# A state-space convolution block on one core: the first output product ahead of the depthwise products, copies of u on ScalarE, and one in_proj visit a pair

## The chip, the cores and the metric

The kernel runs on one core of a Trainium2 chip. The metric is the device time of one execution in microseconds. The core has five engines that run side by side: TensorE (matrix products into eight PSUM banks), VectorE, ScalarE, GpSimd (called Pool here) and SyncE, which issues the DMAs. In the profile they are PE (and PEld for its weight loads), DVE, ACT, POOL and SP.

## The reference

x has the shape (4, 128, 96, 96). It is normalized in 32 groups of channels. Four sequences are then made of every image (rows forward, rows backward, columns forward, columns backward), each goes through the same block, and the four results are put back in place, joined, mixed by a last matrix and added to x:

```python
t = _grouped1x1(x, in_proj_w, in_proj_b, G)
u, gate = (t[:, :HID], t[:, HID:])
u = jax.nn.silu(u)
u = lax.conv_general_dilated(u, dw_w, ..., feature_group_count=HID)   # 5 taps along the sequence
s = _conv1x1(u, ssm_in_w)
a = DMIN + (DMAX - DMIN) * jax.nn.sigmoid(_conv1x1(u, ssm_delta_w, ssm_delta_b))
bb = jnp.tanh(_conv1x1(u, ssm_b_w, ssm_b_b))
cc = jnp.tanh(_conv1x1(u, ssm_c_w, ssm_c_b))
prefix = jnp.cumsum(jnp.log(a), axis=-1)
hst = jnp.exp(prefix) * jnp.cumsum(bb * s * jnp.exp(-prefix), axis=-1)
u = u + _conv1x1(cc * hst + ssm_d[None, :, None] * s, ssm_out_w)
u = _grouped1x1(u * jax.nn.sigmoid(gate), mix_w, mix_b, G)
return _conv1x1(u, out_proj_w, out_proj_b)
```

HID is 256, MH (the width of the state) 32, and a sequence is 9216 long. `hst` is the recurrence h = a h + bb s.

## The kernel before, in words

**Tiling.** A sequence is cut into steps of 16 lines, and each step into four interleaved planes of 384 elements (`N`). A *unit* is one plane of one step of one direction; a *pair* is the two units of the forward and the backward direction, s = 0 and 1, that are worked on together. There are 8 phases (4 images, columns "V" and rows "H"), 6 steps in each and 4 pairs in a step: 192 pairs, t = 0 to 191, and k = t % 4. In the second half of a phase the two directions meet values that the first half has made, so gates and activations are read back from DRAM there.

**The order is written by hand.** Each engine runs its instructions in the order of the program, and the program emits them pair by pair: `pair(t)` for the first six, `pair_on(t)` for the others, then `tail()`. In pair t the front half works on units 2t and 2t + 1 (taps, depthwise products, projections), and the back half on the pair n = t - 6 (`bi` = 2n), whose recurrence is done by then: its ssm_out products, its gating, and, one pair later still, its output products. Everything of one pair is in this order on TensorE:

1. the depthwise products of the first 128 channels, `conv` (band matrices, tile `band`, line 730), into banks 6 and 7;
2. the first output product, `add_next(w[0])` with `accumulate` (line 938, tile `w_fin`), 16 matmul instructions into bank 4; ScalarE copies it to a tile `ys` (line 946, or 944 where a bias is added), and Pool adds that into the accumulator `acc` (line 963). It belongs to the pair before: its operand is the gated v of that pair;
3. in the pairs with k = 0 and 1 ("doubles") the rest of the depthwise products, `conv_less` (tile `less`), into banks 6 and 7 again. In the pairs with k = 2 and 3 ("singles") an addition of an edge row on VectorE (`add_lone`, line 775) takes their place;
4. the second output product, into bank 5;
5. the gate products of the next pair (`gate`, line 630) or the in_proj products of a later step (`new_front`'s `one`, line 492), into banks 4 to 7, mixed with the four `ssm_out` products (`out_of`, line 650) into banks 0 to 3;
6. the projections `proj` (tile `main`), into banks 4 and 5.

**The copies of u.** `under(bi, s)` (line 662) is a ScalarE copy of the unit's u into the two ssm_out banks (0 and 1 for s = 0, 2 and 3 for s = 1), so that the ssm_out product adds to it. A unit that has had this copy is in `seeded`; for others `gating` has an additional VectorE addition (line 710). `gating` (line 711) multiplies the sum by the gate. Banks 0 and 1 are shared with the sum of the taps (`taps`, line 828 on VectorE; the first tap is a ScalarE instruction, line 826), so the taps of one pair, `under(bi, 0)`, the product and the gating take turns in them.

**The early pairs.** In pairs 1 to 5 u is copied out of PSUM by two VectorE copies (line 1012). The in_proj products of the third step come in whole visits, `whole_front(f)`: four products, two Silu instructions (line 505), one over two banks (line 516) and four DMAs of the staged rows (line 523). Visit 8 is in pair 4, visits 9 and 10 in pair 5, and both visits of pair 5 use the banks 6, 7, 2 and 3.

In a phase's course ScalarE's other steps of a pair are the gate's tanh (lines 666, 672) or the Silu of in_proj, and those of `proj`: lines 865, 868, 874 and 886 (`scale_s`).

Of the kernel before, what the change touches and what calls it, by code (L numbers as in the profile page):

```python
# [56 lines left out]
R = 4  # L57
LN = 16
NS = HH // LN
N = LN * WW // R  # L60
# [9 lines left out]
def conv_preact_kernel(  # L70
# [9 lines left out]
    nc = tc.nc  # L80
# [41 lines left out]
    psum = ps.tile([P, 8, 512], F32, name="psum")  # L122
    SSM, TAPS, PROJ = 0, 0, (4, 5)
    FRONT = (7, 6, 2, 3)

    def bank(i):
        return psum[:, i, :]
# [238 lines left out]
    def less_of(p):  # L366
        return 1 if p < 2 else 0
# [172 lines left out]

    def whole_front(i, banks):
        one = new_front(i, banks)
        for s, j in ((0, 1), (0, 0), (1, 0), (1, 1)):
            one(s, j)
        new_silu(i, banks)
        new_stage(i, banks)
        new_rest(i)
# [94 lines left out]
    def ssm(bi, s):  # L642

        k = bi - NU + 8 + s
        return turning[k % 3] if bi >= NU - 8 else SSM + 2 * s
# [13 lines left out]
    def under(bi, s):  # L659

        seeded.add((bi, s))
        nc.scalar.copy(psum[:, ssm(bi, s) : ssm(bi, s) + 2, :N], us[bi][:, s])  # L662
# [50 lines left out]
    us = {}  # L713
# [7 lines left out]
    def blocks(step):  # L721
        return [sils[step][:, s if fresh(step) else 1 - s, 0] for s in range(2)]

    def conv(i, banks, alone=False):

        step, p = units[i]["step"], units[i]["p"]
        sil, k, b0 = blocks(step), less_of(p), min(banks)
        for s in range(2):
            for g in range(4):
                mm(bank(b0 + s), g, band[:, s, p, g, :], columns(step, sil[s][:, g, :], 1 - k),  # L730
                   True, alone)

    def alone(p):
        return p in (0, R - 1)
# [244 lines left out]
    def piece(t, place):  # L979
        later.pop((t % NP, place), lambda: None)()  # L980

    waiting, held = [], []
# [14 lines left out]
    def pair(t):  # L997
        i = 2 * t
        banks = head_banks(t)
        if t == R:  # L1000
            load_lone(1)
        if t:
            new_u(i)
            taps(i, range(1, K))
            single = alone(units[i]["p"])
            conv(i, banks, single)
            if single:
                add_lone(i, banks)
            else:
                conv_less(i, banks, False)  # L1010
                for s in range(2):
                    nc.vector.tensor_copy(us[i][:, s, 0, :], bank(min(banks) + s)[:, :N])
            first_tap(i + 2)
            spots = FRONT if banks == PROJ else (5, 4, 2, 3)
            if t < R:
                front(t + R, spots)
            for f in {4: (8,), 5: (9, 10)}.get(t, ()):
                whole_front(f, (4, 5, 2, 3) if banks != PROJ else (6, 7, 2, 3))
        recurrence(t)
        stats_chunks(t)  # L1020
        load_chunks(t + 2)
        proj(i, banks)
        n, s = divmod(t, 2)
        if n < 2:
            for j in range(2):
                gate(2 * n, s, j, 2 + j)
            for j in range(2):
                tanh_one(n, tile_of(n), s, j, 2 + j)
            load_gate(2 * n + s + UB)
        if t < 2:  # L1030
            keep_silu(0, t)
        if t > 3:
            nc.sync.dma_start(keep(t - 4), tile_of(t - 4))
        if t > 0:
            s = tbs[i - 2][0:64, :]
            nc.gpsimd.tensor_scalar(s, s, d_sb[0:64, 0:1], None, ALU.mult)

    def pair_on(t):
        i, k, n, end = 2 * t, t % R, t - LAG, NU // 2
        bi, last = 2 * n, t == end - 1  # L1040
        late = n > 1 and (n - 1) % (NP * 2) == 0
# [15 lines left out]
        banks, w = (6, 7), PROJ  # L1057
        adder = (nc.vector, True) if last else ()
# [3 lines left out]
            lone[un["step"]] = lone[un["step"] - 1]  # L1062
        elif k == 0 and un["st"] > NS // 2:
            load_lone(un["step"])
        under(bi, 1)
        if k in (1, 3) or late:
            for b, at in reload:
                nc.sync.dma_start(planes(accf, at), planes(xr[b], at))
# [3 lines left out]
        new_u(i)  # L1072
        taps(i, range(1, K))
        conv(i, banks, single)
        if single:
            add_lone(i, banks)
        recurrence(t)
# [4 lines left out]
        for add in held:  # L1082
            add()
        held.clear()
        def add_next(bk):
            if n:
                add = accumulate(waiting.pop(0), bk, *adder)
                held.append(add) if late or k == R - 1 and not last else add()

        add_next(w[0])  # L1090
        if not single:
            conv_less(i, banks, False)
        under(bi, 0)
        if not single:
            copy_u(i, banks)
        add_next(w[1])
        spots = (6, 7, 4, 5)
        if ahead is not None:
            one = new_front(ahead, spots)
# [13 lines left out]
        out_of(bi, 1, 0)  # L1113
        gate_of(0, 1, 5)
        piece(t, 1)
        for s in range(2):
            gating(bi, s)
            if s == 0 and gated is not None:
                for x, y in ((1, 4), (0, 5)):
                    if gated % NP > 1:  # L1120
                        tanh_one(gated, to, x, 1, y)
                    else:
                        spot = to[:, (1 - x - shift) % 5]
                        tanh_into(gated, spot, 1, bank(y)[:, :N])
                        nc.sync.dma_start(keep(gated)[:, x, 1], spot)
            elif s == 0 and ahead is not None:
                new_silu(ahead, spots)
# [335 lines left out]
```

## Time and profile before

| | |
|---|---|
| median of 3 runs | 1733.81 us (1731.57 to 1736.02) |
| the profiled execution | 1736.02 us, span 1734.3 us |
| granted TensorE clock, mean | 0.998 |
| TensorE busy | 1706.6 us |
| VectorE busy | 1506.4 us |
| ScalarE busy | 1479.8 us |
| Pool busy | 1478.3 us |
| HBM read and written | 197.77 MB and 126.70 MB, 187 GB/s over the span |

The span runs from the first to the last instruction of the program; the run's time has 1.7 us around it. A line of the timeline gives the start, the length, the engine, the source line, the operation, the tiles written and read, and how many instructions were merged; in brackets stands the idle time of the engine ahead of it and what ended it. An instruction's length on TensorE is modelled, and the lengths of neighbours overlap, so the distance from one group's start to the next says how long a group takes. A group line has the count after x, then busy time and mean length in ns, then the idle time ahead. Each fp32 matmul appears as two instructions, so four 32-column products into one bank and their second halves give 8 rows, and an output product 16.

### The profile page before, as it was taken

Reading aid. Unit: us, or ns where it says so; the run is one execution under the profiler, and the core shown is the slowest. Engines: PE = TensorE matmul, PEld = TensorE weight load, DVE = VectorE, ACT = ScalarE, POOL = GpSimd, SP = SyncE. Lnnn points to the kernel's source line nnn. Section 1 sums busy time; section 2 is a strip of 40 time slices with the busy share of each in tenths; the row PEclk is TensorE's granted clock in tenths of the full one; section 3 lists DMA queues with packets and bytes.
Section 4 is the critical chain, followed back from the end, with each engine's and each line's share of the span. In section 5 each row is a group of like instructions: output and inputs, shape, how many; then the busy total and the mean of one; then the engine's idle time right before and its main releaser. Section 6 shows DMA issues by size and latency. Waiting matters only on the chain.

```text
span 1734.3 us, 50199 instructions
## 1 busy us (share of the span) xinstructions
PE 1706.6 (98%) x20410; PEld 703.5 (41%) x20410; DVE 1506.4 (87%) x1508; ACT 1479.8 (85%) x2435; POOL 1478.3 (85%) x1455
## 2 busy tenths in 40 slices
PE   7999999999999999999999999999999999999998
PEld 3343344434443434444444434444344433444333
DVE  6799998888889999888888989988888888888897
ACT  4788888888888888888888888888888888888875
POOL 3589898888889988988888988989888889998887
PEclk9999999999999999999999999999999999999999
DMA  7755885358994788337797488733899538753474
GB/s 241 208 169 163 281 242 146 131 197 261 287 289 152 232 245 246 124 132 251 238 306 232 154 275 239 216 117 126 253 287 288 192 119 275 227 167 116 132 239 169
DMA packets 143140, 362.63 MB, mean 209 GB/s; under 512 B 19264, under 2 KB 85696, under 8 KB 142912
## 3 DMA queue, kind: packets, MB, share of 16 engines
q1 hardware_dynamic: 142768, 359.39, 66.7%
q8 instruction: 162, 2.65, 0.7%
q14 instruction: 66, 0.54, 0.1%
q10 hardware_dynamic: 144, 0.04, 0.0%
HBM read 197.77 MB, written 126.70 MB: 187 GB/s over the span
## 4 chain that ended last, share of the span: by engine, by line
PE 89%; DMA 4%; DVE 3%; ACT 2%; issue 1%; POOL 0%; SPq 0%; ACTq 0%; DVEq 0%; POOLq 0%
PE psum L131 72%; PE psum L650 6%; PE psum L630 5%; PE psum L492 5%; DMA kept<-shared 2%; DVE psum L828 1%; DMA sil<-shared 1%; DMA sil<-sil 1%; DVE t L903 1%; DVE u L711 1%; ACT psum L826 1%; DMA acc<-in_xr 0%; PE psum L1274 0%; ACT psum L662 0%; ACT shared L516 0%
## 5 line engine op out<-in xcount | busy, mean ns | idle before, releaser
L828 DVE SCALAR_TENSOR_TENSOR psum<-sil,small,psum 128x768 f32<-128x768 f32 x576 | 589.2, 1023 | 51.6 <-ACT psum L826 34.0
L131 PE MATMUL psum<-u,w_fin 128*32 128x384 f32 (+1 forms) x6192 | 554.6, 485 | 1.1 <-ACT ys L944 0.5
L131 PE MATMUL psum<-u,main 128*32 128x384 f32 x6144 | 537.1, 490 | 1.2 <-ACT shared L672 0.6
L711 DVE SCALAR_TENSOR_TENSOR u<-gate,psum 128x768 f32<-128x768 f32 x376 | 341.9, 951 | 137.9 <-PE psum L650 65.0
L963 POOL TENSOR_TENSOR acc<-ys,acc 128x384 f32<-128x384 f32 x375 | 441.5, 1199 | 12.5 <-ACT ys L944 1.9
L131 PEld LDWEIGHTS psum<-u,w_fin 128*32 128x32 f32 x6192 | 203.1, 109 | 307.9 <-issue 209.3
L131 PEld LDWEIGHTS psum<-u,main 128*32 128x32 f32 x6144 | 180.2, 110 | 328.7 <-issue 207.3
L662 ACT COPY psum<-u 128x768 f32<-128x768 f32 x384 | 306.2, 798 | 7.1 <-DVE u L711 4.3
L909 POOL TENSOR_TENSOR t<-t,t 64x384 f32<-64x384 f32 (+1 forms) x192 | 261.8, 1364 | 45.6 <-DVE t L903 30.8
L131 PE MATMUL psum<-sil,band 128*32 128x384 f32 x3072 | 288.3, 486 | 4.4 <-ACT shared L516 2.2
L876 POOL TENSOR_SCALAR t<-tm 64x384 f32<-64x384 f32 x191 | 180.8, 947 | 125.3 <-ACT tm L865 113.4
L650 PE MATMUL psum<-t,main 32*128 32x384 f32 x1536 | 272.1, 519 | 3.7 <-ACT psum L662 3.0
L910 POOL TENSOR_TENSOR t<-t,t 64x384 f32<-64x384 f32 (+1 forms) x192 | 237.5, 1237 | 15.1
L877 POOL TENSOR_TENSOR t<-t,tm 64x384 f32<-64x384 f32 x192 | 235.6, 1227 | 15.3
L828 DVE SCALAR_TENSOR_TENSOR u<-sil,small,psum 128x768 f32<-128x768 f32 x192 | 194.9, 1015 | 6.8
L946 ACT COPY ys<-psum 128x384 f32<-128x384 f32 x288 | 138.3, 480 | 56.9 <-PE psum L131 46.9
L826 ACT ACTIVATE psum<-sil,small 128x768 f32<-128x768 f32 x191 | 171.7, 899 | 17.5 <-DVE u L711 13.4
L131 PEld LDWEIGHTS psum<-sil,band 128*32 128x32 f32 x3072 | 106.7, 109 | 153.2 <-issue 71.1
L630 PE MATMUL psum<-x_in,wn 32*128 32x384 f32 x768 | 161.0, 497 | 0.0
L492 PE MATMUL psum<-x_in,wn 32*128 32x385 f32 x704 | 149.4, 504 | 2.2 <-ACT sil L505 2.2
L505 ACT ACTIVATE sil<-psum,bnorm 128x385 f32<-128x385 f32 x176 | 102.4, 583 | 48.7 <-PE psum L492 35.5
L666 ACT ACTIVATE gate<-psum,bnorm 128x384 f32<-128x384 f32 x168 | 97.3, 581 | 43.5 <-PE psum L630 25.3
(112 smaller groups left out, 1692.6 us busy)
## 6 DMA issues: line engine op xcount, KB each, us to landing
gate<-kept SPq DMA_DIRECT2D x106, 768.0 KB, 5.6
kept<-gate SPq DMA_DIRECT2D x82, 768.0 KB, 3.7
sil<-sil SPq DMA_DIRECT2D x32, 770.0 KB, 7.9
sil<-shared SPq DMA_DIRECT2D x240, 96.2 KB, 2.8
x_in<-in_xs SPq DMA_DIRECT2D x194, 96.2 KB, 3.2
out<-acc SPq DMA_DIRECT2D x46, 384.0 KB, 7.7
x_in<-in_xs SPq DMA_DIRECT2D x88, 192.5 KB, 5.4
acc<-in_xr SPq DMA_DIRECT2D x39, 384.0 KB, 6.9
```

Of the source, the lines that this page charges most:

```text
L131: nc.tensor.matmul(o[r, : rhs.shape[-1]], lhsT, rhs, start=start, stop=stop, skip_group_check=True)
L492: nc.tensor.matmul(bank(banks[2 * j + s])[:, : N + 1], stats[units[step * UB]["b"]][0][a, s, :], x_in[s][a, q, :], start=True, stop=True,)
L630: nc.tensor.matmul(bank(to)[:, :N], stats[un["b"]][0][r, s, :], x_in[s][r, q, off : off + N], start=True, stop=True)
L650: nc.tensor.matmul(bank(ssm(bi, s) + j)[:, :N], w_so[r, bass.ts(j, P)], z[r, :], start=(bi, s) not in seeded, stop=True, skip_group_check= ...
L662: nc.scalar.copy(psum[:, ssm(bi, s) : ssm(bi, s) + 2, :N], us[bi][:, s])
L711: nc.vector.scalar_tensor_tensor(v, g, 1.0, pz, ALU.add, ALU.mult)
L826: nc.scalar.activation(part, src, AF.Copy, scale=w_tap[:, 0:1])
L828: nc.vector.scalar_tensor_tensor(us[i][:, :, 1, :] if k == K - 1 else part, src, w_tap[:, k : k + 1], part, ALU.mult, ALU.add,)
L877: nc.gpsimd.tensor_mul(ta[0:64, p, :], tb[0:64, :], tm[0:64, :])
L909: engine.tensor_mul(ta[0:64, p, r], tb[64:P, r], ta[64:P, p, r])
L910: engine.tensor_add(tb[0:64, r], ta[0:64, p, r], tb[0:64, r])
L963: adder.tensor_add(part, y, part)
```

## The change

Five things are changed.

- A whole visit issues its four in_proj products in the order (0,1), (1,1), (0,0), (1,0) of (s, j).
- In pairs 4 and 5 one ScalarE copy over two banks takes u out of PSUM, in place of two VectorE copies; pairs 1 to 3 keep these.
- Pairs 4 and 5 have one visit each (8 and 9). Visit 10 moves to pair 6, the first of `pair_on` (n = 0), behind its depthwise products, with the banks 4, 5, 2 and 3. That pair leaves out `under(bi, 1)`, since banks 2 and 3 are in use, and so has the additional VectorE addition for s = 1.
- From pair 7 to 190 the first output product is issued at the very start of the pair, ahead of `under(bi, 1)` and of the depthwise products, into bank 2. Only its matmuls and its copy to `ys` move; `settle` issues Pool's addition where it was. The last pair keeps the old place and bank 4.
- Ahead of the gating VectorE copies one column of u (128x1) onto itself.

```diff
@@ whole_front
-        for s, j in ((0, 1), (0, 0), (1, 0), (1, 1)):
+        for s, j in ((0, 1), (1, 1), (0, 0), (1, 0)):
             one(s, j)
@@ pair
             else:
                 conv_less(i, banks, False)
-                for s in range(2):
-                    nc.vector.tensor_copy(us[i][:, s, 0, :], bank(min(banks) + s)[:, :N])
+                if t < R:
+                    for s in range(2):
+                        nc.vector.tensor_copy(us[i][:, s, 0, :], bank(min(banks) + s)[:, :N])
+                else:
+                    nc.scalar.copy(us[i][:, :, 0, :], psum[:, min(banks) : min(banks) + 2, :N])
             first_tap(i + 2)
             spots = FRONT if banks == PROJ else (5, 4, 2, 3)
             if t < R:
                 front(t + R, spots)
-            for f in {4: (8,), 5: (9, 10)}.get(t, ()):
-                whole_front(f, (4, 5, 2, 3) if banks != PROJ else (6, 7, 2, 3))
+            if t >= R:
+                whole_front(t + R, (4, 5, 2, 3) if banks != PROJ else (6, 7, 2, 3))
@@ pair_on
-        under(bi, 1)
+        def add_next(bk):
+            return accumulate(waiting.pop(0), bk, *adder) if n else None
+
+        def settle(add):
+            if add:
+                held.append(add) if late or k == R - 1 and not last else add()
+
+        first = None if last else add_next(2)
+        if n:
+            under(bi, 1)
...
         conv(i, banks, single)
+        if not n:
+            whole_front(t + R, (4, 5, 2, 3))
         if single:
             add_lone(i, banks)
...
         held.clear()
-        def add_next(bk):
-            if n:
-                add = accumulate(waiting.pop(0), bk, *adder)
-                held.append(add) if late or k == R - 1 and not last else add()
-
-        add_next(w[0])
+        if last:
+            first = add_next(w[0])
+        settle(first)
         if not single:
             conv_less(i, banks, False)
         under(bi, 0)
         if not single:
             copy_u(i, banks)
-        add_next(w[1])
+        settle(add_next(w[1]))
...
         piece(t, 1)
+        corner = us[bi][:, 0, 0, 0:1]
+        nc.vector.tensor_copy(corner, corner)
         for s in range(2):
             gating(bi, s)
```

## The prediction

> **What bounds the kernel now.** I read the spans and clocks first, then the page and the list of waits, then the timeline of single pairs, because the first views leave little to find.
>
> ```profile
> core 0: 1734.3 us, clock 0.998
> ```
> ```profile
> PE 1706.6 (98%) x20410; PEld 703.5 (41%) x20410; DVE 1506.4 (87%) x1508; ACT 1479.8 (85%) x2435; POOL 1478.3 (85%) x1455
> ...
> PE 89%; DMA 4%; DVE 3%; ACT 2%; issue 1%; POOL 0%; SPq 0%; ACTq 0%; DVEq 0%; POOLq 0%
> ```
> ```profile
> PE psum L131 <- ACT shared L672: 2.6, 4, 1.3
> PE psum L131 <- ACT shared L516: 2.2, 6, 1.0
> ```
>
> TensorE is busy for 98% of the span and carries 89% of the chain that ended last. The waits that the list gives it are few: 2.6 and 2.2 us, at the start of a pair's depthwise products. But a busy TensorE is modelled with overlapping ends, so a short wait between two groups does not show as idle time. It shows in the distance from one group to the next. Here is one pair in full (pair 11, the second of two "single" pairs), from one pair's projections to the next.
>
> ```profile
> 115.78 2.79 PE L131 MATMUL psum<-u,main 128*32 128x384 f32 x32
> ...
> 118.39 1.48 PE L131 MATMUL psum<-sil,band 128*32 128x384 f32 x16
> ...
> 119.68 2.77 PE L131 MATMUL psum<-u,w_fin 128*32 128x384 f32 x32
> ...
> 119.73 0.62 ACT L886 ACTIVATE t<-t,small 64x384 f32<-64x384 f32 x1
> ...
> 120.26 0.79 ACT L662 COPY psum<-u 128x768 f32<-128x768 f32 x1
> ...
> 120.53 1.01 DVE L828 SCALAR_TENSOR_TENSOR u<-sil,small,psum 128x768 f32<-128x768 f32 x1
> ...
> 121.22 0.48 ACT L946 COPY ys<-psum 128x384 f32<-128x384 f32 x1 [0.17 <-PE psum L131]
> ...
> 121.59 0.81 ACT L662 COPY psum<-u 128x768 f32<-128x768 f32 x1
> ...
> 122.37 0.58 PE L630 MATMUL psum<-x_in,wn 32*128 32x384 f32 x1
> ...
> 122.54 0.60 PE L650 MATMUL psum<-t,main 32*128 32x384 f32 x3
> ...
> 123.58 1.82 DVE L711 SCALAR_TENSOR_TENSOR u<-gate,psum 128x768 f32<-128x768 f32 x2 [0.18 <-PE psum L650]
> ...
> 124.04 2.79 PE L131 MATMUL psum<-u,main 128*32 128x384 f32 x32
> ...
> 124.68 0.90 ACT L826 ACTIVATE psum<-sil,small 128x768 f32<-128x768 f32 x1
> ```
> A "double" pair (one with the `less` products), two pairs earlier, for the same place:
> ```profile
> 105.94 0.58 PE L630 MATMUL psum<-x_in,wn 32*128 32x384 f32 x1
> ...
> 105.94 0.60 PE L650 MATMUL psum<-t,main 32*128 32x384 f32 x3
> ...
> 107.52 2.79 PE L131 MATMUL psum<-u,main 128*32 128x384 f32 x32
> ```
>
> In the double pair the gate product (L630) and the three ssm_out products (L650) start together and the projections follow 1.58 us later. In the single pair L650 starts 0.17 us after L630 and the projections follow 1.67 us after. What L650 waits for stands just above: ScalarE's second copy of u into the ssm_out banks (L662, `under(bi, 0)`) ends at 121.59 + 0.81 = 122.40. So a single pair (8.26 us from 115.78 to 124.04) is set by ScalarE, and it is 0.09 us over what TensorE needs. ScalarE in turn loses 0.17 us in that pair, waiting with its copy of the first output product (L946), which stands between the two copies of u. That idle time is what the reordering can remove.
>
> There is a second thread into the same copy. `under(bi, 0)` writes banks 0 and 1, where the taps are summed, so it also waits for VectorE's last tap, which ends at 120.53 + 1.01 = 121.54, 0.05 us before the copy starts. The same two events in pair 10 (the first single pair), and in pair 51, where the output products' copy adds a bias:
>
> ```profile
> 112.19 1.01 DVE L828 SCALAR_TENSOR_TENSOR u<-sil,small,psum 128x768 f32<-128x768 f32 x1
> ...
> 113.33 0.81 ACT L662 COPY psum<-u 128x768 f32<-128x768 f32 x1
> ```
> ```profile
> 471.47 1.01 DVE L828 SCALAR_TENSOR_TENSOR u<-sil,small,psum 128x768 f32<-128x768 f32 x1
> ...
> 472.15 0.59 ACT L944 ACTIVATE ys<-psum,b_fin 128x384 f32<-128x384 f32 x1 [0.17 <-PE psum L131]
> ...
> 472.63 0.81 ACT L662 COPY psum<-u 128x768 f32<-128x768 f32 x1
> ...
> 473.31 0.59 PE L492 MATMUL psum<-x_in,wn 32*128 32x385 f32 x1
> ...
> 473.58 0.60 PE L650 MATMUL psum<-t,main 32*128 32x384 f32 x3
> ```
>
> Tap to copy: 113.33 - 113.20 = 0.13 us, and 472.63 - 472.48 = 0.15 us. With the bias L650 is 0.27 us late, because the copy takes 0.59 instead of 0.48.
>
> **The first output product ahead (pairs 7 to 190; pair 191 keeps the old order).** Sixteen matmuls (about 1.29 us, 118.39 to 119.68) move from behind the depthwise products to ahead of them, from bank 4 to bank 2, and their copy moves ahead of both copies of u. TensorE's work is the same. New waits: the product needs bank 2, which the second gating of the pair before reads until 123.58 + 1.82 = 125.40, while TensorE comes free at 124.04 + 2.61 = 126.65. It doesn't wait; everything of TensorE would queue behind it. The copy to ys needs the product, ready near 118.39 + 1.48 = 119.87, while ScalarE ends L886 only at 120.35: no wait either, and both copies of u stand behind it. The pair's add of the edge row now follows depthwise products that end at 119.68 + 1.48 = 121.16, before the tap at 121.54 lets VectorE go. The Pool adds keep their place, no DMA is moved, and ys has four buffers.
>
> So ScalarE's 0.17 us go and the copy can start earlier, until the tap holds it. How soon after a tap a waiting ScalarE starts is seen in the early rows below: 66.41 + 1.01 = 67.42 to 67.46, that is 0.04. Left to gain are then 0.13 - 0.04 = 0.09 in the first single pair, 0.05 - 0.04 = 0.01 in the second, and TensorE's own pace allows 0.09. Of 88 single pairs (7 to 183), 24 have the bias (two of four in the second half of each H phase, 12 fours). The other 32 fours: 32 x 0.10 = 3.2 us. With the bias I take 0.17 (ScalarE's idle) in the first and 0.15 - 0.04 = 0.11 in the second: 12 x 0.28 = 3.4. Bounds for these two terms: nothing, if another ScalarE step fills the hole; and 88 x 0.09 plus 24 x 0.10 (0.27 against 0.17 of lateness) = 10.3, if the tap moves up too. I take 6.6, what the tap leaves.
>
> **Waits at the start of a pair.** The 4.8 us of the two waits in the list above lie ahead of the depthwise products, because ScalarE still reads banks 6 and 7. The first output product now runs in that time (1.29 us covers all but the longest). But where ScalarE is very late it is late again at the end of the pair, as in the pair with the 1.3 us wait:
>
> ```profile
> 1036.50 0.81 ACT L662 COPY psum<-u 128x768 f32<-128x768 f32 x1
> ...
> 1037.45 0.60 PE L650 MATMUL psum<-t,main 32*128 32x384 f32 x3
> ```
>
> L650 starts 0.14 after the copy ends at 1037.31, so that pair returns only ScalarE's hole, 0.2 us, and so does the one with 1.0. The rest, 2.5 us, I count in full: 2.9 us, between 0.4 and 4.8.
>
> **Pairs 4 to 6.** Here the span has its worst stretch.
>
> ```profile
> 65.11 0.88 PE L131 MATMUL psum<-sil,less 64*32 64x384 f32 x16
> ...
> 66.41 1.01 DVE L828 SCALAR_TENSOR_TENSOR u<-sil,small,psum 128x768 f32<-128x768 f32 x1
> ...
> 67.46 0.91 ACT L826 ACTIVATE psum<-sil,small 128x768 f32<-128x768 f32 x1 [2.43 <-DVE u L828]
> ...
> 69.03 2.92 PE L492 MATMUL psum<-x_in,wn 32*128 32x385 f32 x8 [2.18 <-ACT sil L505]
> ...
> 71.88 4.65 PE L131 MATMUL psum<-u,main 128*32 128x384 f32 x32
> ...
> 72.03 0.58 ACT L505 ACTIVATE sil<-psum,bnorm 128x385 f32<-128x385 f32 x1 [0.74 <-PE psum L492]
> ...
> 72.52 0.90 ACT L516 ACTIVATE shared<-psum,bnorm 128x770 f32<-128x770 f32 x1
> ...
> 80.88 2.79 PE L131 MATMUL psum<-u,main 128*32 128x384 f32 x32
> ```
> ```profile
> 68.90:75.60 6.70, 6.57 (x32) 2.20 (x36) 5.39 (x5) 3.30 (x6) 2.87 (x3) 0.50 0.92 259
> ```
>
> Pair five's second visit of in_proj waits 2.18 us for the first one's banks, the granted clock is then 0.50 for 6.7 us (the eighth column of the stretch), and 32 projections take 4.65 us instead of 2.79. After the change pair five has one visit. ScalarE copies u (0.8) as soon as the `less` products end, near 66.2 with ScalarE's longer queue of pair four (its copy of 0.8 now stands ahead of the first tap; VectorE in return is freed of two copies). So the projections of pair five start near 67.1, not 71.88, and end near 69.8. The depthwise products of pair six follow (1.5), then the moved visit (0.9), near 72.2. Its first two products go to banks 2 and 3, free by then. ScalarE then has two L505 (0.58), one L516 (0.90) and the one copy left of pair six (0.81), about 2.6 us after 72.1: 74.8. L650 follows, and the projections 1.5 us later at 76.4, against 80.88: 4.5 us. The four sil DMAs of the visit are issued in pair six behind pair five's stores of gates; they are first read by pair eight, about 10 us on. The copy that pair six leaves out (ScalarE 0.8) comes back as an add on VectorE between the two gatings, like one L711 of 1.82 / 2 = 0.91. That pushes pair seven's taps past the 0.21 us that VectorE has there, and costs 0.6: net 3.9 us, between 1.2 (no half clock in another run) and 4.5.
>
> The Trainium skill, in "TensorE: Matmul & The Clock Gate" (the practical table at its end), says that the clock stays up unless TensorE idles for about 3 us. By that rule the gap would not have halved the clock; here 2.18 us of idle time stood right before it, so the measurement decides, and the shorter gap left in pair six is a risk, below.
>
> **The corner copy.** One VectorE copy of 128x1 a pair, ahead of the gating, on 186 pairs. The nearest row:
>
> ```profile
> L243 DVE COPY mean<-psum 128x1 f32<-128x1 f32 x3 | 0.5, 152 | 0.0
> ```
>
> VectorE idles 0.18 us just there (the row of 123.58), waiting for L650, and the corner waits only for the copy of u that ended at 122.40. So I take nothing. Below nothing it can be a few hundredths, since it takes one wait off L711; above, 0.15 and a restart of 0.04 where VectorE has no idle time. ScalarE's first tap (124.68) could bear 124.68 - 124.49 - 0.04 = 0.15 of that, with the first gating ending near 123.58 + 0.91.
>
> **The sum.** 3.2 + 3.4 + 2.9 + 3.9 = 13.4 us against the profiled execution, whose time is 1736.02 (span 1734.3): 1722.6. That run is 2.2 over the median of the three shown, 1733.81. If the others lack the half clock, their base and my early term shrink together, so the changed kernel comes out the same: I write 1722.
>
> **The rivals.** *Half clock again.* TensorE idles about 1.7 us in pair six behind the moved visit, with another short gap before L650. If the clock is halved there too, 32 projections cost 4.65 - 2.79 = 1.9 more and their neighbours up to 0.8: 1725. For it: 2.18 us sufficed. Against: the mean clock of 0.998 stands for 3.5 us lost in the span, and this one stretch (half of 6.7) uses that up, so the waits of 1.3 us elsewhere left the clock alone. 0.15.
>
> *The single pairs don't move.* If the tap follows the copy so closely everywhere, or ScalarE finds another wait, both terms of the steady pairs fall away: 1736.0 - 6.8 = 1729. The 0.05 of pair 11 speaks for it, the 0.13 and 0.15 against. 0.15.
>
> *TensorE's pace throughout*, taps included, and the start waits nearly whole: 10.3 + 4.3 + 3.9 gives 1717.5. 0.13.
>
> *Slower: the corner lands on VectorE's path.* If in most pairs VectorE reaches the corner with no idle time left, each gating starts 0.19 later, the first tap on ScalarE with it, then the four taps, the copy of u and L650. It decides from the point where the delay exceeds 0.15. In the doubles there is a scan ahead of the gating, and there it is likeliest. In all 186 pairs it would be 35 us; in half of them, 17.7, less the 6.8 of the early pairs and the start waits: 1747. Against it: TensorE has slack in the doubles. 0.07.
>
> **How the numbers follow.** The forecast has 0.50. The range 1714 to 1730 reaches over the half clock, the unmoved single pairs and TensorE's pace, with the bounds of the start waits; what it leaves out is the corner and the tails. About 0.3% (5.2 us) is what a measurement of this kernel can tell from no change. Faster by more: 0.50 + 0.15 + 0.13 and half of the unmoved case: 0.85. Within: 0.08. Slower: 0.07.
>
> **What would show it.** Right: L650 starting with L630 in the first single pairs, and 0.02 or less sooner than now in the second of an unbiased four, with the tap 0.04 ahead of the copy; L946 of the first product with no wait on TensorE; projections of pair six near 76.4; the waits on L672 and L516 at or below 0.5 us. Wrong: L711 with the corner ahead of it and no idle time; a longer distance between projections in the doubles than 9.11; the first output product waiting for L711; a clock of 0.50 after 72 us.

## The result, and the profile after

The changed kernel takes 1746.51 us (median of 8 runs, 1742.61 to 1753.97), against 1735.53 for the kernel before in as many runs. The ratio is 1.0065, 95% interval [1.0046, 1.0085]: 0.65% slower, where 0.8% faster was forecast. The profiled execution took 1742.61 us, the fastest of the eight, so the traces account for 6.3 us of the 11.0 by which the medians differ (spans 1740.6 and 1734.3). Its clock, its busy times and the shares of its chain:

```profile
core 0: 1740.6 us, clock 0.999
```
```profile
PE 1716.3 (99%) x20410; PEld 684.0 (39%) x20410; DVE 1547.0 (89%) x1691; ACT 1500.6 (86%) x2436; POOL 1453.6 (84%) x1455
...
PE 93%; DMA 2%; ACT 2%; DVE 1%; issue 1%; POOL 1%; SPq 0%; ACTq 0%; DVEq 0%; POOLq 0%
```

In the list of waits, the 2.6 and 2.2 us on L672 and L516 at the start of a pair have shrunk to 0.5. Beside that TensorE's products wait 3.2 us for the copy of u (3.0 before) and once 1.9 for L516, in pair six:

```profile
PE psum L650 <- ACT psum L662: 3.2, 6, 0.6
PE psum L492 <- ACT shared L516: 1.9, 1, 1.9
PE psum L131 <- ACT shared L672: 0.5, 1, 0.5
```

By these views nothing is lost. VectorE is busy for 40.6 us more, and that is the lead. The groups of its scan and of the corner, and of GpSimd's product L877, before:

```profile
L877 POOL TENSOR_TENSOR t<-t,tm 64x384 f32<-64x384 f32 x192 | 235.6, 1227 | 15.3
L903 DVE TENSOR_TENSOR_SCAN t<-t 64x768 f32<-64x768 f32 x56 | 116.6, 2082 | 1.8
```

and after:

```profile
L877 POOL TENSOR_TENSOR t<-t,tm 64x384 f32<-64x384 f32 x192 | 208.8, 1087 | 15.3
L903 DVE TENSOR_TENSOR_SCAN t<-t 64x768 f32<-64x768 f32 x56 | 135.2, 2414 | 2.0 <-POOL t L877 0.2
L1128 DVE COPY u<-u 128x1 f32<-128x1 f32 x186 | 27.8, 150 | 15.0 <-ACT psum L662 4.3
```

The corner's 27.8 us were known. The scan, which the change does not touch, takes 18.6 us more, and L877 takes 26.8 less. A step has two scans, one in each double (k = 0 and 1). Here are VectorE and GpSimd in a double with k = 0 (two lines) and in the one with k = 1 behind it, before:

```profile
94.93 3.18 DVE L903 TENSOR_TENSOR_SCAN t<-t,t 64x768 f32<-64x768 f32 x1
98.15 1.82 DVE L711 SCALAR_TENSOR_TENSOR u<-gate,psum 128x768 f32<-128x768 f32 x2
...
103.56 0.94 POOL L876 TENSOR_SCALAR t<-tm 64x384 f32<-64x384 f32 x1
104.30 1.81 DVE L903 TENSOR_TENSOR_SCAN t<-t 64x768 f32<-64x768 f32 x1
104.58 2.33 POOL L877 TENSOR_TENSOR t<-t,tm 64x384 f32<-64x384 f32 x1
...
105.94 0.58 PE L630 MATMUL psum<-x_in,wn 32*128 32x384 f32 x1
...
107.05 1.82 DVE L711 SCALAR_TENSOR_TENSOR u<-gate,psum 128x768 f32<-128x768 f32 x2 [0.94 <-PE psum L650]
```

and after, from the same double with k = 0 to the gate products of the single behind it (pair 10):

```profile
91.62 3.11 DVE L903 TENSOR_TENSOR_SCAN t<-t,t 64x768 f32<-64x768 f32 x1
...
94.83 0.15 DVE L1128 COPY u<-u 128x1 f32<-128x1 f32 x1
...
95.10 1.82 DVE L711 SCALAR_TENSOR_TENSOR u<-gate,psum 128x768 f32<-128x768 f32 x2
...
96.09 0.91 ACT L826 ACTIVATE psum<-sil,small 128x768 f32<-128x768 f32 x1 [0.47 <-DVE u L711]
...
101.21 1.01 POOL L877 TENSOR_TENSOR t<-t,tm 64x384 f32<-64x384 f32 x1
101.25 2.58 DVE L903 TENSOR_TENSOR_SCAN t<-t 64x768 f32<-64x768 f32 x1
...
102.47 0.58 PE L630 MATMUL psum<-x_in,wn 32*128 32x384 f32 x1
...
103.93 0.15 DVE L1128 COPY u<-u 128x1 f32<-128x1 f32 x1
104.20 1.82 DVE L711 SCALAR_TENSOR_TENSOR u<-gate,psum 128x768 f32<-128x768 f32 x2
105.19 0.91 ACT L826 ACTIVATE psum<-sil,small 128x768 f32<-128x768 f32 x1 [0.45 <-DVE u L711]
...
109.30 1.01 DVE L828 SCALAR_TENSOR_TENSOR u<-sil,small,psum 128x768 f32<-128x768 f32 x1
...
110.64 0.91 PE L630 MATMUL psum<-x_in,wn 32*128 32x384 f32 x2
111.30 0.94 PE L650 MATMUL psum<-t,main 32*128 32x384 f32 x8
```

Read it in this order. In the first double VectorE goes from scan to gating without a pause. There the corner costs 0.33 us: it starts 0.10 after the scan's end (94.73), takes 0.15, and L711 starts 0.12 behind it, where L711 alone started 0.04 behind the scan (98.11). The first tap on ScalarE (L826) waits 0.47 for that gating. Everything VectorE does next is late, and the scan of the second double comes to its start 0.04 us *after* GpSimd has begun L877, where before it came 0.28 *ahead* of it. The two don't run together: with the scan ahead, the scan took 1.81 and L877 2.33; with L877 ahead, L877 took 1.01 and the scan 2.58. So a delay of 0.33 has become one of about 1.1, the 0.77 that the scan takes longer included. The second corner adds its 0.33. The gating of the second double begins 1.73 us after the gate products there (102.47 to 104.20), where before it was 1.11 (105.94 to 107.05), of which VectorE sat idle for 0.94. That makes the first tap (L826) late and the last one behind it (L828): it ends at 110.31, ScalarE's second copy of u (L662) at 111.16, and L650 starts 0.66 us behind L630 in the single pair, where it was 0.17.

The Trainium skill, in "SBUF — State Buffer", section "SBUF: two separate sides", states this rule: VectorE's instructions with two SBUF inputs and GpSimd's instructions that read SBUF share a pair of ports as "an exclusive lock, not a bandwidth split"; who starts first holds it for the whole instruction and the other blocks. The durations above agree with it: the scan reads two tensors, and so does L877. The order in the records is not exact to a few hundredths, though: in pairs 117 and 165 the scan's record starts 0.04 and 0.01 us ahead of L877's, and the scan takes 2.65 and 2.63 all the same.

To see which pairs lose, the starts of the projections are taken from a trace and the distances from one pair's to the next are summed by k (pairs 8 to 183, 44 of each k; the seven distances from the first pair's projections to pair seven's stand in the first column). The last column has the second scans, 48 of them: how many start while L877 runs, and their sum. All in us.

| kernel | first seven | k=0 | k=1 | k=2 | k=3 | second scans |
|---|---|---|---|---|---|---|
| before | 54.1 | 406.8 | 404.1 | 365.8 | 368.5 | 16, 96.9 |
| after | 51.4 | 401.6 | 404.8 | 375.8 | 372.0 | 35, 115.3 |

The changes add up to +6.3 us, as much as the spans differ. The loss is +10.0 in the first singles (k = 2): 22 of the 44 take more than 8.5 us, where 8.26 was usual and one did before.

### The profile page after: what moved, and what is told of

Read it like the earlier page. It is cut to its first block, busy times and chain, and to the rows that moved or that the text cites. A ratio compares the mean times of both kernels' runs of the same rounds, so it can differ in the third digit from the quotient of the medians.

```text
span 1740.6 us, 50158 instructions
## 1 busy us (share of the span) xinstructions
PE 1716.3 (99%) x20410; PEld 684.0 (39%) x20410; DVE 1547.0 (89%) x1691; ACT 1500.6 (86%) x2436; POOL 1453.6 (84%) x1455
## 4 chain that ended last, share of the span: by engine, by line
PE 93%; DMA 2%; ACT 2%; DVE 1%; issue 1%; POOL 1%; SPq 0%; ACTq 0%; DVEq 0%; POOLq 0%
PE psum L131 74%; PE psum L650 7%; PE psum L492 6%; PE psum L630 5%; DMA sil<-sil 1%; DMA kept<-shared 1%; DMA sil<-front 1%; DVE psum L828 1%; DMA acc<-in_xr 0%; PE psum L1287 0%; ACT psum L662 0%; DVE u L711 0%; DVE u L828 0%; ACT tm L865 0%; ACT psum L826 0%
## 5 line engine op out<-in xcount | busy, mean ns | idle before, releaser
L828 DVE SCALAR_TENSOR_TENSOR psum<-sil,small,psum 128x768 f32<-128x768 f32 x576 | 589.1, 1023 | 58.7 <-ACT psum L826 38.6
L131 PE MATMUL psum<-u,w_fin 128*32 128x384 f32 (+1 forms) x6192 | 567.2, 485 | 0.9 <-DVE acc L961 0.3
L711 DVE SCALAR_TENSOR_TENSOR u<-gate,psum 128x768 f32<-128x768 f32 x376 | 342.1, 951 | 85.3 <-PE psum L650 72.9
L131 PEld LDWEIGHTS psum<-u,w_fin 128*32 128x32 f32 x6192 | 190.5, 109 | 320.3 <-issue 251.4
L662 ACT COPY psum<-u 128x768 f32<-128x768 f32 x383 | 297.4, 801 | 13.8 <-DVE u L711 4.3
L131 PE MATMUL psum<-sil,band 128*32 128x384 f32 x3072 | 283.4, 486 | 0.0
L650 PE MATMUL psum<-t,main 32*128 32x384 f32 x1536 | 259.0, 522 | 4.5 <-ACT psum L662 3.2
L877 POOL TENSOR_TENSOR t<-t,tm 64x384 f32<-64x384 f32 x192 | 208.8, 1087 | 15.3
L828 DVE SCALAR_TENSOR_TENSOR u<-sil,small,psum 128x768 f32<-128x768 f32 x192 | 194.9, 1015 | 6.8
L826 ACT ACTIVATE psum<-sil,small 128x768 f32<-128x768 f32 x191 | 171.9, 900 | 31.6 <-DVE u L711 30.4
L630 PE MATMUL psum<-x_in,wn 32*128 32x384 f32 x768 | 161.9, 497 | 0.0
L131 PEld LDWEIGHTS psum<-sil,band 128*32 128x32 f32 x3072 | 98.8, 110 | 149.9 <-issue 114.0
L946 ACT COPY ys<-psum 128x384 f32<-128x384 f32 x288 | 138.0, 479 | 21.7 <-PE psum L131 15.2
L903 DVE TENSOR_TENSOR_SCAN t<-t 64x768 f32<-64x768 f32 x56 | 135.2, 2414 | 2.0 <-POOL t L877 0.2
```

Of the source, the lines that this page charges most:

```text
L131: nc.tensor.matmul(o[r, : rhs.shape[-1]], lhsT, rhs, start=start, stop=stop, skip_group_check=True)
L630: nc.tensor.matmul(bank(to)[:, :N], stats[un["b"]][0][r, s, :], x_in[s][r, q, off : off + N], start=True, stop=True)
L650: nc.tensor.matmul(bank(ssm(bi, s) + j)[:, :N], w_so[r, bass.ts(j, P)], z[r, :], start=(bi, s) not in seeded, stop=True, skip_group_check= ...
L711: nc.vector.scalar_tensor_tensor(v, g, 1.0, pz, ALU.add, ALU.mult)
L828: nc.vector.scalar_tensor_tensor(us[i][:, :, 1, :] if k == K - 1 else part, src, w_tap[:, k : k + 1], part, ALU.mult, ALU.add,)
L877: nc.gpsimd.tensor_mul(ta[0:64, p, :], tb[0:64, :], tm[0:64, :])
```

## The experiments

The letters a to d ran together on one chip (before: 1733.93 us), e to h on another (1734.57), j and k later on that one (1732.64), and i last on a third (1734.16). Theory A puts the loss on the corner and the order of scan and L877; B on the output product ahead; C on the early pairs. The expectations of j and k count 41 of the 44 pairs of k = 2; the other three take about 25 us.

**a: without the corner.**

```diff
-        corner = us[bi][:, 0, 0, 0:1]
-        nc.vector.tensor_copy(corner, corner)
```


> The changed kernel without the corner copy, all else as changed. Theory A (the corner copy costs VectorE about 0.33 us ahead of the gating of a double pair, that pushes the next double's scan behind Pool's product L877, the scan takes 0.77 longer, and the first single pair's ssm_out product comes 0.48 late): the loss goes, about 1725 us, 0.993 of the kernel before, and the scans of k = 1 take 1.8 us again. Theory B (the product ahead of the depthwise products is itself the loss, by ScalarE's or TensorE's order): stays near 1745, 1.006. Theory C (the early pairs lose): stays near 1745.

Measured: 1734.43 us, ratio 0.9998 [0.9981, 1.0014]. The corner is the whole loss against before. The other four edits together are worth nothing that these runs can tell, though theory A had given them 9 us (1725).

**b: the corner alone, on the kernel before.**

```diff
         piece(t, 1)
+        corner = us[bi][:, 0, 0, 0:1]
+        nc.vector.tensor_copy(corner, corner)
```


> The kernel before with the corner copy alone. Theory A: slower, 1745 to 1752 (1.006 to 1.010), with scans of 2.5 us in the second double pair of the V phases and ssm_out products some 0.5 us late in the first single pair. Theory B and C: 1735 to 1737, within 0.2% of before.

Measured: 1739.84 us, 1.0034 [1.0019, 1.0048]. The corner loses alone too, but half as much (theory A had 1745 to 1752), and at another place: k = 1 grows by 5.3 us (table below) and k = 2 by 1.2. The scans flip as in the changed kernel (37 of 48). The timeline of b has, at the start of the second double, a wait that the product ahead covers in the changed kernel: the depthwise products' weights wait for the tanh L672, which stands behind the late first tap. In b's list of waits TensorE's products wait for it 1.2 us in six places, before in none; that this makes up all of the 5.3 is not shown.

```profile
98.54 0.91 ACT L826 ACTIVATE psum<-sil,small 128x768 f32<-128x768 f32 x1 [0.30 <-DVE u L711]
99.38 0.89 ACT L672 ACTIVATE gate<-psum,bnorm 128x768 f32<-128x768 f32 x1
...
100.32 0.16 PEld L131 LDWEIGHTS psum<-sil,band 128*32 128x32 f32 x8 [0.67 <-ACT gate L672]
```

**c: the first output product ahead, alone, and d: the edits of pairs 4 to 6, alone**, each on the kernel before.

```diff
# c
+        first = None if last else add_next(2)
...
-        add_next(w[0])
+        settle(first)
# d
+                    nc.scalar.copy(us[i][:, :, 0, :], psum[:, min(banks) : min(banks) + 2, :N])
...
+        if not n:
+            whole_front(t + R, (4, 5, 2, 3))
```


> The kernel before with the first output product ahead in bank 2 alone: no corner copy, early pairs as before. Theory A: a small gain, 1727 to 1731 (0.995 to 0.998), most of it in the pairs with a bias and at the waits for L672 and L516. Theory B: 1745 or more. Theory C: 1735 or less.

> The kernel before with the edits of pairs 4 to 6 alone (copies of u on ScalarE, one visit each, visit 10 in pair 6 and its missing copy into banks 2 and 3). Theory A and B: 1731 to 1734 (0.997 to 0.999), the eighth pair's projections 2 to 4 us sooner. Theory C: 1740 or more.

Measured: c 1736.28 us, 1.0012 [0.9999, 1.0024]; d 1731.45 us, 0.9980 [0.9967, 0.9993]. The product ahead gains nothing alone either, where 1727 to 1731 was expected. The early edits alone are a gain of about 3.5 us, and d is the one version here that beats both kernels. Its eighth pair starts its projections 1.6 us sooner (52.5 for 54.1 in the tables), where 2 to 4 was expected.

**e and f: the corner only where k = 0, and only where k = 1.**

```diff
-        nc.vector.tensor_copy(corner, corner)
+        if k == 0:    # f: k == 1
+            nc.vector.tensor_copy(corner, corner)
```


> The changed kernel with the corner only in the first double of each step (k = 0), where VectorE runs from tap to gating without idle time. Theory A (the delay before that gating pushes the next double's scan behind GpSimd's L877, and the scan then takes 2.5 us in place of 1.8): about 35 of the 48 second scans start behind L877 as with the corner everywhere (15 without it), their sum is 113 to 116 us in place of 98, and the time is 1740 to 1745. Rival P (no jump; each corner in a double is a plain delay of the same size): about half of the 12 us, 1739 to 1741, and with the corner in the second double alone as much. Rival S (the loss lies in the singles, where the corner stands before the gating): 1734, as without the corner.

> The changed kernel with the corner only in the second double of each step (k = 1), behind the second scan. Theory A: the next scan is three pairs away, so no more than some 15 to 18 of the 48 second scans start behind L877 and their sum stays at 98 to 101 us; what is left is the tap of the third pair up to 0.3 us later: 1735 to 1738. Rival P (plain delays): 1739 to 1741, as with the corner in the first double. Rival S (singles): 1734.

Measured: e 1737.0 us, 1.0013 [1.0001, 1.0024]; f 1734.78, 0.9999 [0.9988, 1.0011]. In e the scans flip as theory A had it (33 of 48, 113.2 us):

```profile
L903 DVE TENSOR_TENSOR_SCAN t<-t 64x768 f32<-64x768 f32 x56 | 133.3, 2380 | 1.9 <-POOL t L877 0.2
```

But the time did not follow: theory A had 1740 to 1745, and the two rivals' 1739 to 1741 and 1734 were missed as well. The time of f lies between theory A's 1735 to 1738 and rival S's 1734 and does not tell them apart; its scans stay as they are without a corner (15 of 48, 97.9 us). So the flip alone is not the loss, and theory A as first put was too simple. In e's pair 9 the gating starts 104.86 - 103.46 = 1.40 us behind the gate products, without idle time, and in pair 10 L650 starts 0.31 behind L630:

```profile
103.46 0.58 PE L630 MATMUL psum<-x_in,wn 32*128 32x384 f32 x1
...
104.86 1.82 DVE L711 SCALAR_TENSOR_TENSOR u<-gate,psum 128x768 f32<-128x768 f32 x2
...
111.65 0.58 PE L630 MATMUL psum<-x_in,wn 32*128 32x384 f32 x1
111.96 0.60 PE L650 MATMUL psum<-t,main 32*128 32x384 f32 x3
```

Without a corner (a) VectorE has 0.84 us of idle time there, and the gating comes 1.10 behind the gate products, which start at 103.11:

```profile
104.21 1.82 DVE L711 SCALAR_TENSOR_TENSOR u<-gate,psum 128x768 f32<-128x768 f32 x2 [0.84 <-PE psum L650]
```

The flip and the first corner eat that, the gating is 0.30 later, and L650 only 0.1 (a: 0.20). The next 0.33 us, the second corner's, have nothing left to eat.

**g: the product ahead in the doubles only, without the corner.**

```diff
-        first = None if last else add_next(2)
+        early_product = not last and not single
+        first = add_next(2) if early_product else None
...
-        if last:
+        if not early_product:
             first = add_next(w[0])
...
-        corner = us[bi][:, 0, 0, 0:1]
-        nc.vector.tensor_copy(corner, corner)
```


> The changed kernel without the corner, with the first output product ahead in the doubles only; the singles have it where the kernel before has it. Theory C1 (by the sums over the pairs: the product ahead takes 4 us off the pairs that are first doubles and 1 off the second ones, and puts 5 on the fourth pairs, whose ScalarE copies come late): the singles' 5 us come back, 1728 to 1731. Rival C2 (the gain in the first double is only the loss in the single before it, told from another edge): the two go together, 1732 to 1735.

Measured: 1732.85 us, 0.9994 [0.9981, 1.0006]. The time lies in C2's range, but is told apart neither from a nor from before. The sums of its trace do not decide it: k = 0 stays at 403.0, as C1 has it, and the usual single is back at 8.26 us, but k = 3 is at 375.1, because of a few pairs in which ScalarE was late behind a DMA (TensorE's products wait 8.1 us in ten places for the tanh L672, where before has 2.6 in four). This one is inconclusive.

**h: GpSimd's two operations in the other order in the first double, corner and all.**

```diff
+        swapped = i // 2 % R == 0
+        if swapped:
+            nc.gpsimd.tensor_mul(ta[0:64, p, :], tb[0:64, :], tm[0:64, :])
         if not by_scalar:
             nc.gpsimd.tensor_scalar(*decay(i))
-        nc.gpsimd.tensor_mul(ta[0:64, p, :], tb[0:64, :], tm[0:64, :])
+        if not swapped:
+            nc.gpsimd.tensor_mul(ta[0:64, p, :], tb[0:64, :], tm[0:64, :])
```


> The changed kernel, corner and all, with GpSimd's two operations behind the projections in the other order in the first double of each step: the product of two tensors (L877) first, the one with one tensor and two constants (L876) behind it. No work is left out. Theory A (the scan and the product of two tensors don't run together): the product is over some 0.95 us sooner and the second scan starts behind or beside L876; if L876 doesn't hold a scan, the second scans sum to 88 to 100 us and the time is 1733 to 1738. If L876 holds a scan as well: 1743 to 1747 with the scans at 113 to 116. Rival P (a plain delay of 0.4 us before the gating is the whole loss): 1743 to 1747, with the scans shorter all the same.

Measured: 1738.04 us, 1.0025 [1.0011, 1.0039]. About 60% of the loss is gone with the corner still on all 186 pairs. VectorE's order and work are untouched, so a plain delay by the corner is not the whole loss. The number lies between the two cases that I had set out, and the scan shows why. It is now held by the one-input operation (L879 here), but for less:

```profile
100.63 0.93 POOL L879 TENSOR_SCALAR t<-tm 64x384 f32<-64x384 f32 x1
100.71 2.25 DVE L907 TENSOR_TENSOR_SCAN t<-t 64x768 f32<-64x768 f32 x1
```

The second scans sum to 104.3 us, between 98.2 (a) and 115.3. That takes only some 0.23 us from each, but k = 2 falls from 375.8 to 369.8: again more than in proportion, as with room that has just run out.

**j: the corner in both doubles, in no single, and k: the corner everywhere, the product ahead in the doubles only.** After e the theory was the threshold: neither corner costs much, both do. (j's diff is e's, with `k < 2`; k's is g's on the changed kernel.)

> The changed kernel with the corner in both doubles of a step and in no single. With the corner in the first double alone the time was 1737.0, in the second alone 1734.8, without it 1734.4 and everywhere 1746.5: the parts sum to 1737.4, 9 us short. Theory T (a threshold: the scan's 0.7 us use up VectorE's room ahead of the third pair's tap, and the 0.3 of the second double's corner come on top of that): the third pairs take 348 to 351 us in sum as in the changed kernel, and the time is 1744 to 1747. Rival S (the corner in the singles costs the rest, at its own place): 1736 to 1739, third pairs 342 to 344.

> The changed kernel, corner and all, with the first output product ahead in the doubles only. Theory T1 (with the product ahead the second double no longer waits at its start for ScalarE's tanh, so TensorE comes to the third pair at its full pace and meets the late tap there): the second doubles stay at 403 to 406 us in sum, the third pairs at 348 to 351, 1743 to 1747. Rival T2 (it is the product ahead in the third pair itself that makes it wait for the tap): the third pairs fall to 341 to 344, 1736 to 1739.

Measured: j 1743.75 us, 1.0070 [1.0058, 1.0083]; k 1740.7, 1.0062 [1.0044, 1.0081]. In j the pairs of k = 2 take 377.0 us and 22 of them more than 8.5, as in the changed kernel; the corner in the singles costs nothing. In e the excess over a in k = 2 is 2.4 us, in f 1.1, in j 11.1. In k the pairs of k = 2 stay at 375.7, though their own product is not ahead: T1 holds, and the late tap is what they meet. (k's time is 2.3 us under the 1743 that I gave, beside a kernel before that was 1.9 faster there.)

| kernel | first seven | k=0 | k=1 | k=2 | k=3 | second scans |
|---|---|---|---|---|---|---|
| a no corner | 51.4 | 402.8 | 403.2 | 365.9 | 373.7 | 15, 98.2 |
| b corner alone | 53.2 | 407.1 | 409.4 | 367.0 | 365.0 | 37, 112.6 |
| c product ahead alone | 54.7 | 402.0 | 402.9 | 366.6 | 375.5 | |
| d early edits alone | 52.5 | 406.1 | 403.8 | 366.6 | 365.4 | |
| e corner, k = 0 | 51.3 | 404.0 | 405.6 | 368.3 | 372.2 | 33, 113.2 |
| f corner, k = 1 | 52.6 | 402.6 | 403.3 | 367.0 | 373.9 | 15, 97.9 |
| g ahead in doubles | 52.7 | 403.0 | 402.8 | 365.9 | 375.1 | |
| h GpSimd swapped | 50.2 | 402.6 | 405.5 | 369.8 | 372.5 | 104.3 in sum |
| j corner, k = 0, 1 | 51.3 | 403.2 | 405.0 | 377.0 | 373.3 | 32, 114.1 |
| k corner, ahead in doubles | 51.3 | 401.7 | 404.4 | 375.7 | 371.6 | 36, 114.7 |

**i: why the product ahead gains nothing: bank 4 in place of bank 2.** In a's trace of pair 11 ScalarE no longer waits for TensorE, and still it is no sooner:

```profile
116.93 0.61 ACT L886 ACTIVATE t<-t,small 64x384 f32<-64x384 f32 x1
117.57 0.48 ACT L946 COPY ys<-psum 128x384 f32<-128x384 f32 x1
118.08 1.53 ACT L662 COPY psum<-u 128x768 f32<-128x768 f32 x2
...
117.72 1.01 DVE L828 SCALAR_TENSOR_TENSOR u<-sil,small,psum 128x768 f32<-128x768 f32 x1
...
119.57 0.58 PE L630 MATMUL psum<-x_in,wn 32*128 32x384 f32 x1
119.76 0.60 PE L650 MATMUL psum<-t,main 32*128 32x384 f32 x3
```

Before, the first L662 started at 120.26, 0.09 us before L886 ended (120.35), and the second at 121.59, 0.11 before L946 ended (121.70). Here L946 starts 0.03 *behind* L886 and L662 0.03 behind L946: the copy of u writes bank 2, which the ys copy has just read, so ScalarE waits for itself. From the end of L886 to the second L662 it was 121.59 - 120.35 = 1.24; it is 118.81 - 117.54 = 1.27 (the second copy starts one copy of 0.80 before the end of the merged two).

```diff
-        first = None if last else add_next(2)
+        first = None if last else add_next(w[0])
...
-        corner = us[bi][:, 0, 0, 0:1]
-        nc.vector.tensor_copy(corner, corner)
```


> The changed kernel without the corner, with the first output product ahead as there but in bank 4 (a bank of the projections) in place of bank 2. Measures why ScalarE gained nothing: with the product in bank 2 the copy of u into banks 2 and 3 (L662) starts 0.03 us behind the end of the ys copy (L946) that reads bank 2, while copies that share no bank start 0.06 to 0.10 before the end of the one ahead of them. Theory B2 (the shared bank makes ScalarE wait for itself): with bank 4 that L662 starts some 0.1 before the end of L946, and from the end of L886 to the second L662 it is about 1.15 in place of 1.28. Rival B3 (ScalarE gets no overlap behind a copy that waited for TensorE): L662 stays 0.03 behind, 1.28. In both the time is worse, since bank 4 is read by the tanh L865 until some 0.25 us behind the end of the projections and TensorE waits for that in nearly every pair: 180 pairs by 0.1 to 0.25, 1750 to 1780.

Measured (without the corner): 1761.57 us, 1.0149 [1.0122, 1.0176]. The time is TensorE's wait for the tanh L865, as expected: its weight loads wait for it in 184 places, in a in three.

```profile
PEld psum L131 <- ACT tm L865: 141.6, 184, 1.5
```

The mechanism is in the timeline of the same pair:

```profile
117.67 0.62 ACT L886 ACTIVATE t<-t,small 64x384 f32<-64x384 f32 x1
118.31 0.48 ACT L946 COPY ys<-psum 128x384 f32<-128x384 f32 x1
118.68 1.56 ACT L662 COPY psum<-u 128x768 f32<-128x768 f32 x2
...
120.53 0.58 PE L630 MATMUL psum<-x_in,wn 32*128 32x384 f32 x1
120.54 0.60 PE L650 MATMUL psum<-t,main 32*128 32x384 f32 x3
```

L662 starts 0.11 before the end of L946 again, the second at 119.44, 1.15 behind L886's end, and L650 starts with L630. Over the 144 places where L662 follows L946 the median is 0.10 us of overlap before and in i, and 0.03 of gap in a and in the changed kernel. B2 holds for that step. L946 starts 0.02 behind L886 in a, in the changed kernel and in i alike, so bank 2 is not the reason there; what is stays open. The Trainium skill, in "ScalarE: Activation LUTs", section "What ACT_TABLE_LOAD costs", gives an overlap of about 93 ns for neighbouring activations; the trace agrees for the copies of u in the kernel before (0.09 to 0.11), and shows these two cases in which it is not there.

## Why the prediction was wrong, point by point

- **The corner, "So I take nothing": failed, and it decides the case.** The 0.18 us of idle time were read in a single pair and carried to all 186. In the singles it holds (j). In the first double, where the scan stands ahead of the gating, VectorE had none, and the price was 0.33, not the 0.15 and 0.04 set as the upper bound: the corner pays a gap on both its sides. What the prediction lacked altogether is what a delay does to the *next* pair: it turns the order of scan and L877 around, and 0.3 becomes 1.1.
- **The slower rival named the right place and the wrong account.** It had the doubles behind the scan, but as 0.19 for each pair delayed, with "TensorE has slack in the doubles" against it. That is true: k = 0 and k = 1 did not lose. The delay went through them and came out in the single behind, and not in proportion: 1.1 and 2.4 us for one corner, 11.1 for both. That its 1747 lies beside the measured 1746.51 is luck: it has 93 gatings late by 0.19 each, and the runs show 22 singles late by some 0.45. Its chance of 0.07 came from looking for the wait in the pair that causes it.
- **The single pairs (6.6 us): failed.** The step that failed is "So ScalarE's 0.17 us go and the copy can start earlier". The 0.17 did go. But in the new order ScalarE's copies lose the overlap that they had: 0.14 us at L662, by bank 2, and 0.12 where L946 now follows L886 in L662's place; 0.07 of it comes back where the two copies of u now overlap. The usual distance in a is 8.29 us against 8.26 before; with the bias 8.39 (k = 2) and 8.49 (k = 3) against 8.36. The count was off too: of the 88 singles of pairs 8 to 183, 18 have the bias, not 24. The rival "the single pairs don't move, if ScalarE finds another wait" was right, at 0.15.
- **The waits at the start of a pair (2.9): the waits went, the time did not.** In a and after the k = 0 pairs are 4 to 5 us shorter, but k = 3 is 3.5 to 5.2 longer, of which the step above explains 2 (35 x 0.03 and 9 x 0.13). The places where ScalarE is late behind a DMA now show at the end of the pair. That was seen for two pairs, and counted in full for the rest.
- **Pairs 4 to 6 (3.9): right in kind, 2.7 in size.** The first seven distances fell from 54.1 to 51.4, and d alone gains. Pair six's projections start at 77.18, not 76.4: the half clock came again, as the rival had it, behind 1.92 us of idle time, though it fell on the in_proj and ssm_out products and the projections took 2.90 and not 4.65.

```profile
73.52 1.15 PE L492 MATMUL psum<-x_in,wn 32*128 32x385 f32 x2 [1.92 <-ACT shared L516]
...
77.18 2.90 PE L131 MATMUL psum<-u,main 128*32 128x384 f32 x32
```
```profile
74.00:75.00 1.00, 1.00 (x6) 0.56 (x8) 0.15 (x1) 0.46 (x2) 0.98 (x1) 0.53 0.98 384
75.00:76.00 1.00, 1.00 (x11) 0.65 (x6) 0.00 (x0) 0.29 (x1) 0.95 (x1) 0.50 0.80 289
76.00:77.00 1.00, 1.00 (x6) 0.09 (x3) 0.95 (x1) 0.00 (x0) 0.92 (x2) 0.50 0.85 216
```

The granted clock (the third column from the end) is 0.5 for some 3 us. How long it is 0.5 differs from trace to trace behind the same idle time, and the first seven distances with it. For 6.8 us of it they take 54.1 and 54.7 us without the early edits (before, c) and 52.5 to 52.7 with them (d, f, g); for 3.4 us, 53.2 without (b) and 51.3 or 51.4 with them (a, e, j, k and the changed kernel). So the edits themselves are worth about 2 us, and the rest of the 2.7 is a shorter half clock. Only in h did the clock stay at 1.00 behind its 1.92 us of idle time: there the sum is 50.2, which is 3.9 less than before as forecast, and pair six's projections start at 76.44.

- **The signs.** Of those set out for "right", two came: no wait of the first L946 on TensorE, and waits on L672 and L516 of 0.5. L650 starting with L630 did not come, nor pair six at 76.4. Of those for "wrong", the corner ahead of L711 without idle time came, and the clock of 0.50 after 72 us. The doubles kept a usual distance of 9.11 and 9.13 (9.26 and 9.14 before).

In half of the first singles (22 of 44) the loss is not there, though the scans flip in 35 of 48 steps. The traces of a and of the changed kernel show where the two part. In pairs 9 to 29, 61 to 77, 109 to 125 and 157 to 173 with k = 1 (21 steps; their back half lies in a column phase) the second scan takes 1.81 us in a and ends 1.13 to 1.32 us before its pair's projections start. In the changed kernel it takes 2.53 to 2.65 and ends 0.18 to 0.35 before them, and the single behind each takes 8.68 to 8.80 us. In the other 23 steps between them and up to pair 181 the scan still ends 0.88 us or more ahead, although it starts while L877 runs in 14 of them, the same 14 as in the kernel before; all but one of the singles behind them stay under 8.45. In e the scan ends 0.18 to 0.36 before the projections in 19 of the 21 steps, and without a corner behind it the singles take 8.35 to 8.48. So the flip alone does not decide: the loss stands where the scan ends late against TensorE and a corner follows. Left open: why the row phases leave it more room, and whether there is a place for the product ahead that shares no bank with the copies of u and is free in time.

## What to carry to other kernels

A small instruction is free only where its engine idles in *every* kind of pair that runs it, so look at one timeline of each kind, above all behind the longest instruction of that engine. Where two engines can't run an instruction of theirs together, look at which comes first now and by how much: here a lead of 0.28 us was lost, and a delay of 0.33 became about 1.1. And moving a step out of a wait pays only if the step does not pick up a dependency, such as a shared bank, with its new neighbour on the same engine.

## What the runs showed of the hardware

- A scan of 64x768 on VectorE and a product of two 64x384 tensors on GpSimd hold each other up: 1.81 and 2.33 us with the scan ahead, 2.58 and 1.01 with the product ahead. A one-input GpSimd operation holds the scan too (2.25 us behind 0.93).
- The ScalarE copy L662 behind the copy L946 overlaps it by 0.10 us (median of 144 places), and starts 0.03 behind its end where it writes a bank that L946 has read.
- A VectorE copy of 128x1 takes 0.15 us, and with the gaps around it 0.33 us where VectorE is busy.
- The granted clock fell to 0.50 behind 2.18 us (before) and 1.92 us (after) of idle time on TensorE, for 6.8 and 3.4 us. In h it stayed at 1.00 behind the same 1.92.
